# A graph attention layer and a neighbour quantile layer on one core: attention blocks of 4, 12 and 16 tiles, ordered by hand

## The chip, the core and the metric

The kernel runs on one core of a Trainium2 chip. The metric is the device time of one execution in microseconds (us), as the median of several runs. The engines of the core are TensorE (PE, matmuls; PEld is its weight load), VectorE (DVE), ScalarE (ACT), GpSimd (POOL) and SyncE (SP). Each works through its own queue of instructions in order, and waits on semaphores that the others raise. DMAs are issued from the queues of SP, ACT and POOL. A gather or scatter by a list of indices (an indirect DMA) is always issued from POOL.

## What is computed

There are 4096 nodes with 128 features, and a random adjacency matrix in which a node has about 32 neighbours. Layer 0 is a graph attention layer with eight heads; layer 1 takes quantiles over neighbours. Cut to what matters:

```python
Wh = jnp.einsum('nd,hde->hne', nodes, W)
f1 = jnp.einsum('hnd,hd->hn', Wh, a1)
f2 = jnp.einsum('hnd,hd->hn', Wh, a2)
e = leaky_relu(f1[:, :, None] + f2[:, None, :], 0.2)
att = softmax(jnp.where(adj > 0, e, -9e15), axis=-1)
h = elu(jnp.einsum('hnm,hmd->hnd', att, Wh))
x1 = layernorm(nodes + elu(concat_heads(h) @ W1 + b1)) * gamma + beta
# layer 1: of each node's neighbours every skip-th is dropped,
# the rest are sorted feature by feature
svals = jnp.sort(where(keep, x1, big), axis=1)
agg = (svals[1/4] + svals[1/2] + svals[3/4]) / 3    # places worked out from the count
out = (0.5 * agg + 0.5 * x1) @ Wl.T + bl + x1
```

Since only some 32 of the 4096 columns of a row count, the kernel makes a list of each node's neighbours and works on gathered rows.

## The kernel before

A tile is 128 nodes, so there are 32 tiles. The work has four parts.

**Search** (`neighbours`, L532). For each tile, the 128 rows of the adjacency matrix are loaded in two halves of 2048 columns (L541, a DMA of 1 MB from ACT's queue). ACT turns a half into signs in bf16 and counts them (L547). DVE multiplies each stretch of 512 by a falling ramp (L568), takes the eight largest of each 128 columns (L573), and then eight rounds of the eight largest of all candidates (L585), with these struck out after each round (L587). The result is a list of up to 64 neighbours in a record, `rec`. The function is a generator that yields after each stretch, in pieces, 12 for a tile.

**Records and ranks** (`complete_records`, `rank_by_count`). When all tiles of a block are searched, their lists are completed, all nodes of the block are ranked by their neighbour count, and the records are scattered in that order to DRAM (`rec_d`, L194, from POOL). So the tiles that attention sees have neighbours of nearly equal count, and `CAPS` holds the largest count of each.

**Attention**, tile by tile in that order. `fetch_rows` (L755) reads a tile's records back (`R`, and for narrow layers `list` and `score`, from SP's queue), lets DVE turn the lists and the f1 scores for gathering (L776 to L799), and issues one gather for each slot of the list (L185, POOL), as many as the cap rounded up to four: 24 to 64 for a tile. `weigh_rows` (L816) computes the weights (L825 to L827), spreads them (`pf`, L839), multiplies and sums the gathered rows on PE into `y` (L860), copies y to `raw` on ACT (L871), divides (L875 to L878) and transposes (`yT`, L887, L888). When 2 or 4 tiles are weighed, `transform` (L895) does the two dense layers with their ELU, and the layer norm, for them; the resulting rows `x1` are put on the list `store` and scattered to `x1_d` (L194, named x_d in the profile).

**Sort** (`quantile_out`). For each tile the x1 rows of kept neighbours are gathered, and a selection network of DVE minima and maxima (L1133) with ACT copies (L1129) finds the quantiles. It begins when all x1 rows are stored.

Attention and search overlap. The 32 tiles are handled in three blocks (`BLOCKS`), here of 2, 8 and 22. Block 0 is searched first, with nothing beside it but the set-up. While the tiles of block 0 are in attention, block 1 is searched; while block 1 is in attention, block 2 is searched; block 2 is in attention alone. The function `step` does one tile: it fetches tile i, scatters the stores that are waiting, and weighs tile i-1, with a share of the `transform` of earlier tiles and, between the yields of `weigh_rows`, a share (`quota`) of the search pieces.

What sets the order: inside `tc.manual_schedule(engines=ORDERED)`, DVE, PE and ACT run their instructions in the order in which the program writes them, and POOL's order is chosen by a planner with estimated times. This holds in blocks 0 and 1. In block 2 there is no such context, so the planner orders all engines. SP is always the planner's. The sort is ordered by hand on all engines.

Buffers that matter: gathered rows `G` have two buffers (a tile whose cap is over 44 takes two of them; the surplus over 32 of a smaller cap goes to `Gs`), and in block 2 a third, since every third is taken from another pool (`take`, L744). `R` has 5 buffers, in block 2 8. `sgn` has two, `adj_t` three. `y` has four PSUM banks (`YBANKS`), `x1` one buffer.

In block 2 the records of all tiles are scattered once more to `all_d`, in an order over all nodes, four tiles' scatters in each of the first eight steps; in the middle of the block they are read back to make the lists of the sort (`kept_rows`).

Of the kernel before, what the change touches and what calls it, by code (L numbers as in the profile page):

```python
# [9 lines left out]
F32 = mybir.dt.float32  # L10
# [7 lines left out]
ORDERED = {mybir.EngineType.DVE, mybir.EngineType.PE, mybir.EngineType.Activation}  # L18
ALL = ORDERED | {mybir.EngineType.Pool}

P = 128
# [22 lines left out]
    2: [33, 61],  # L44
    8: [27, 29, 31, 33, 34, 37, 40, 61],
    22: [
        24, 25, 26, 27, 28, 29, 30, 30, 31, 32, 32, 33, 34, 34, 35, 36, 37, 38, 39, 40, 43, 63,
    ],
# [5 lines left out]
BLOCKS = [2, 8, 22]  # L54
# [10 lines left out]
YBANKS = 4  # L65
# [143 lines left out]
def kernel(  # L209
# [132 lines left out]
    def step(fetch=None, pieces=None, quota=0, size=2, more=None):  # L342
        if fetch:
            weigh.append(fetch_rows(tc, pools, narrow[turn[0] % 2], *fetch, xt_d, bad, uses))
            turn[0] += 1
        while store:
            scatter(nc, x1_d, *store.pop(0))
        if len(weigh) > 1 or (weigh and not fetch):
            R, parts = weigh.pop(0)
            place = len(members)  # L350
            members.append(R)
            turns = len(parts) + 13
            each = -(-quota // turns)
            done = 0
            for _ in weigh_rows(tc, attp, pools, pp, parts, turned, place, size, consts):
                if tails and next(tails[0], True):
                    tails.pop(0)
                for _ in range(min(each, quota - done)):
                    next(pieces, None)
                    done += 1  # L360
            quota -= done
            if len(members) == size:
                tails.append(
                    transform(tc, attp, pp, more, turned.pop(0), list(members), consts, store)
                )
                members.clear()
        elif not fetch:
            while tails:
                if next(tails[0], True):
                    tails.pop(0)  # L370
        for _ in range(quota):
            next(pieces, None)

    t0 = 0
    for b, n in enumerate(BLOCKS):
# [5 lines left out]
        if last:  # L381
# [12 lines left out]
            for i in range(n):  # L394
                step((recs_d[b], i, CAPS[n][i], t0 + i), size=2 if i in (0, n - 1) else 4, more=kp)
                for t in waiting[:4]:
                    scatter(nc, all_d, rec[:, t, 0:REC1], ranks[:, t : t + 1])
                waiting = waiting[4:]
                if i == n // 2:
                    R = cp.tile([P, NT, REC1], F32, name="all", bufs=1)  # L400
                    nc.sync.dma_start(R, all_d.rearrange("(t p) w -> p t w", p=P))
                    kept_rows(tc, cp, R, jp1, pidx, idx, own_i, bad, limits)
                    slot_places(tc, cp, R, picks, limits)
        else:
            pieces = search(t0 + n, BLOCKS[b + 1])
            quota = -(-BLOCKS[b + 1] * PIECES // n)
            with tc.manual_schedule(engines=ORDERED):
                for i in range(n):
                    step((recs_d[b], i, CAPS[n][i], t0 + i), pieces, quota, more=kp)
                for _ in pieces:  # L410
                    pass
        t0 += n
    for _ in range(3):
        step(size=2, more=kp)
    count_bad(tc, cp, kp, bad, ones, total)
# [116 lines left out]
def neighbours(tc, adjp, rec, num, adj, tiles, back, chunk):  # L532
# [11 lines left out]
    def sign():  # L544
        t, i, cnt, adj_t = loads.pop(0)
        sgn = adjp.tile([P, half], BF16, name="sgn", bufs=2)
# [9 lines left out]
    sign()  # L556
    while signs:
# [5 lines left out]
        if i == 0:  # L563
            first = adjp.tile([P, NCH * 8], F32, name="first")
        for b in range(half // 512):

            key = sgn[:, ts(b, 512)].rearrange("p (c w) -> p c w", w=CW)
            nc.vector.tensor_tensor(  # L568
                key, key, back.unsqueeze(1).to_broadcast([P, 512 // CW, CW]), ALU.mult
            )  # L570
            c0 = i * half + b * 512
            for c in range(512 // CW):
                nc.vector.max(first[:, ts(c0 // CW + c, 8)], key[:, c, :])  # L573
            yield
# [17 lines left out]
def complete_records(tc, cp, rec, num_all, bad, jp1, pidx, t0, n):  # L592
# [3 lines left out]
    for a in range(t0, t0 + n, step):  # L596
# [12 lines left out]
        has = tmp("has")  # L609
# [134 lines left out]
def take(pools, shape, name, turn, bufs=2):  # L744
# [10 lines left out]
def fetch_rows(tc, ap, narrow, rec_d, i, cap, t, xt_d, bad, turn):  # L755
# [3 lines left out]
    R = take(ap, [P, REC], "R", turn, 5)  # L759
# [21 lines left out]
    G, col = None, 0  # L781
    for s0, w in layers(cap):
        k = P // w
        idx = ap[0].tile([P, 32], I32, name="idx", bufs=6)
# [7 lines left out]
        if w < 32 or f1x32 is None:  # L792
# [5 lines left out]
            f1x = ap[0].tile([P, 32 * H], F32, name="f1x", bufs=6)  # L798
# [3 lines left out]
        f1v = f1x.rearrange("p (h g) -> p g h", h=H)[:, 0:w, :]  # L802
        if w == 32:
# [12 lines left out]
def weigh_rows(tc, ap, pools, pp, parts, turned, place, size, consts):  # L816
# [16 lines left out]
    for half in range(2):  # L833
# [61 lines left out]
def transform(tc, ap, pp, more, yT, members, consts, store):  # L895
# [54 lines left out]
    x1 = ap.tile([P, 4, D], F32, name="x1", bufs=1)[:, 0:m, :]  # L950
# [432 lines left out]
```

## Time and profile before

| | us |
|---|---|
| median of 3 runs | 3860.11 (3859.21 to 3861.66) |
| the profiled execution, its own time | 4473.73 |
| its span, first to last instruction | 4471.8 |
| PE busy | 815.7 (18%) |
| DVE busy | 2634.2 (59%) |
| ACT busy | 1265.3 (28%) |
| POOL busy | 2284.8 (51%) |
| gathers of attention (G and Gs), POOL | 1060.0 (x1092) and 89.6 (x92) |
| gathers of the sort (vals), POOL | 911.9 (x960) |
| minima and maxima of the sort (L1133, vals), DVE | 1403.0 |

The span is from the first to the last instruction of one profiled execution. Busy time counts instructions at work, not waiting. In a line of the timeline, the first number is the start from the span's beginning, the second how long the merged instructions took; the brackets give the idle time of the engine ahead of them and what ended it: another engine's instruction, a DMA, "issue" (nothing that the profile shows), or "remote" (a semaphore whose raiser it could not name). In a line of waits stand the total in us, the number of waits, and the longest. The profiled execution is longer than the plain runs, by 613.6 us.

### The profile page before, as it was taken

Reading aid. Unit: us, or ns where it says so; the run is one execution under the profiler, and the core shown is the slowest. Engines: PE = TensorE matmul, PEld = TensorE weight load, DVE = VectorE, ACT = ScalarE, POOL = GpSimd, SP = SyncE. Lnnn points to the kernel's source line nnn. Section 1 sums busy time; section 2 is a strip of 40 time slices with the busy share of each in tenths; the row PEclk is TensorE's granted clock in tenths of the full one; section 3 lists DMA queues with packets and bytes.
Section 4 is the critical chain, followed back from the end, with each engine's and each line's share of the span. In section 5 each row is a group of like instructions: output and inputs, shape, how many; then the busy total and the mean of one; then the engine's idle time right before and its main releaser. Section 6 shows DMA issues by size and latency. Waiting matters only on the chain. (4 is left out here: it accounts for less than half of the span.)

```text
span 4471.8 us, 18412 instructions
## 1 busy us (share of the span) xinstructions
PE 815.7 (18%) x2751; PEld 469.4 (10%) x2753; DVE 2634.2 (59%) x5147; ACT 1265.3 (28%) x2352; POOL 2284.8 (51%) x2452
## 2 busy tenths in 40 slices
PE   2001212223231413332425110000000001000101
PEld 1000110111121201111112000000000000000001
DVE  5665667767111205110212436888878999999897
ACT  2112222222010213121213213333333444443433
POOL 1332343454657465756663575666565334455530
PEclk9955555555565656655656555555555555555555
DMA  5313333231222121212221111111111001111110
GB/s 168 105 48 111 97 101 96 91 93 43 54 46 53 36 57 41 55 47 48 48 51 28 40 53 39 47 45 47 40 45 41 22 21 30 31 38 35 36 28 3
DMA packets 115233, 241.18 MB, mean 54 GB/s; under 512 B 51904, under 2 KB 68288, under 8 KB 106912
## 3 DMA queue, kind: packets, MB, share of 16 engines
q0 software_dynamic: 76224, 161.01, 14.2%
q10 hardware_dynamic: 12160, 68.49, 4.5%
q1 hardware_dynamic: 26720, 10.41, 1.2%
q14 instruction: 103, 0.84, 0.1%
q8 instruction: 26, 0.43, 0.0%
HBM read 228.56 MB, written 11.18 MB: 54 GB/s over the span
## 5 line engine op out<-in xcount | busy, mean ns | idle before, releaser
L1133 DVE TENSOR_TENSOR vals<-low,vals 128x1024 f32<-128x1024 f32 (+9 forms) x1359 | 1403.0, 1058 | 338.9 <-ACT low L1129 129.8
L185 POOL DMA_INDIRECT G<-xt_d,idx x1092 | 1060.0, 971 | 736.3 <-issue 480.8
L185 POOL DMA_INDIRECT vals<-x_d,idx x960 | 911.9, 950 | 295.4 <-issue 287.5
L1129 ACT COPY low<-vals 128x1024 f32<-128x1024 f32 (+10 forms) x701 | 607.4, 876 | 968.6 <-DVE vals L1133 621.1
L871 ACT COPY raw<-y 32x129 f32<-32x129 f32 (+1 forms) x928 | 239.2, 258 | 854.6 <-remote 516.9
L860 PE MATMUL y<-G,pf 128*64 128x258 f32 (+1 forms) x1200 | 289.9, 518 | 978.3 <-issue 574.9
L1143 PE MATMUL st_ps<-ident,u 128*128 128x128 f32 x344 | 87.1, 437 | 1781.4 <-ACT u L1142 1377.9
L194 POOL DMA_INDIRECT out_dram<-o,own_i x32 | 31.8, 992 | 626.0 <-ACT o L1155 623.7
L875 DVE TENSOR_SCALAR rden<-raw 128x8 f32<-128x8 f32 x32 | 6.2, 194 | 550.5 <-ACT raw L871 407.0
L573 DVE MAX8 first<-sgn 128x8 f32<-128x128 bf16 x1024 | 223.9, 281 | 152.4 <-remote 121.5
L1143 PEld LDWEIGHTS st_ps<-ident,u 128*128 128x128 f32 x344 | 76.0, 327 | 1792.3 <-ACT u L1142 1385.4
L860 PEld LDWEIGHTS y<-G,pf 128*64 128x64 f32 (+1 forms) x1200 | 141.5, 191 | 1111.7 <-issue 861.6
L547 ACT ACTIVATE sgn<-adj_t 128x2048 bf16<-128x2048 int32 x64 | 122.1, 1907 | 303.0 <-DVE first L573 177.0
L908 DVE TENSOR_SCALAR e<-e 128x512 f32<-128x512 f32 x64 | 28.0, 437 | 242.4 <-ACT e L935 131.8
L194 POOL DMA_INDIRECT x_d<-x,R x32 | 32.9, 1027 | 260.2 <-DVE x L974 235.6
L888 ACT COPY yT<-turned 128x512 f32<-128x512 f32 x64 | 65.6, 1026 | 302.6 <-PE turned L887 157.2
L839 DVE TENSOR_TENSOR pf<-z,own 128x512 f32<-128x512 f32 x124 | 80.6, 683 | 112.1 <-issue 87.5
L887 PE MATMUL turned<-ident,raw 128*128 128x128 f32 x256 | 68.6, 420 | 391.6 <-DVE raw L878 233.1
L916 PE MATMUL o<-hv,W_sb 128*128 128x256 f32 (+1 forms) x176 | 93.8, 650 | 229.6 <-DVE hv L910 118.5
L1133 DVE TENSOR_TENSOR most<-low,most 128x1024 f32<-128x1024 f32 (+7 forms) x116 | 131.9, 1167 | 2.6 <-issue 0.5
L185 POOL DMA_INDIRECT Gs<-xt_d,idx x92 | 89.6, 974 | 85.7 <-remote 30.0
L585 DVE MAX8 rec<-first 128x8 f32<-128x256 f32 x256 | 109.3, 427 | 35.8 <-remote 18.7
(180 smaller groups left out, 1774.7 us busy)
## 6 DMA issues: line engine op xcount, KB each, us to landing
adj_t<-in_adj_dram ACTq DMA_DIRECT2D x64, 1024.0 KB
G<-xt_d,idx POOLq DMA_INDIRECT x1092
vals<-x_d,idx POOLq DMA_INDIRECT x960
R<-rec_d SPq DMA_DIRECT2D x128, 26.4 KB
xt_d<-rec SPq DMA_DIRECT2D x4, 548.0 KB
score<-rec_d SPq DMA_DIRECT2D x132, 1.0 KB
rec<-in_x_dram SPq DMA_DIRECT2D x4, 512.0 KB
Gs<-xt_d,idx POOLq DMA_INDIRECT x92
```

Of the source, the lines that this page charges most:

```text
L185: nc.gpsimd.indirect_dma_start(out=dst, out_offset=None, in_=rows, in_offset=bass.IndirectOffsetOnAxis(ap=idx, axis=0),)
L547: nc.scalar.activation(sgn, adj_t, AF.Sign, accum_out=cnt[:, i : i + 1])
L573: nc.vector.max(first[:, ts(c0 // CW + c, 8)], key[:, c, :])
L585: nc.vector.max(top, first)
L839: nc.vector.tensor_tensor(pf.rearrange("p (g k h) -> p g k h", g=g2, k=k), z[:, ts(half, g2), :].unsqueeze(2).to_broadcast(spread), own[w] ...
L860: nc.tensor.matmul(yv[p0 : p0 + m], lhsT=pf[:, c : c + m], rhs=rhs, start=(i == 0), stop=(i == len(parts) - 1), skip_group_check=True,)
L871: nc.scalar.copy(raw[p0 : p0 + m, 4 * half + b, :], yv[p0 : p0 + m, a, :])
L887: nc.tensor.transpose(t_ps[:, b, :], yn[:, 4 * half + b, :], ident)
L916: nc.tensor.matmul(o, lhsT=consts["W1_sb"][:, h, :], rhs=hv[:, ts(j, n)], start=(h == 0), stop=(h == H - 1),)
L1129: nc.scalar.copy(kept, low)
L1133: nc.vector.tensor_tensor(high if end else low, kept, high, ALU.max if end else ALU.min)
L1143: nc.tensor.matmul(st_ps, lhsT=u, rhs=ident, start=(i == 0), stop=(i == len(terms) - 1))
```

## The change

The blocks become 4, 12 and 16 tiles, with caps of their own. `fetch_rows` is split in two: `list_rows` reads the records and makes the lists on DVE, and the new `fetch_rows` only issues the gathers. The lists of tile i+1 are written ahead of the step of tile i. All four compute engines are ordered by hand, in all three blocks; the last three steps and `count_bad` are moved into the ordered part. The multiply of the search (L568) handles a half row of 2048 at once in place of four times 512. `y` takes two banks at a time, and ACT copies two of its rows in one instruction, half as many copies. `sgn` has three buffers, and two halves are signed ahead. `x1` is taken from a pool by group size; `R`, `idx` and `f1x` have more buffers; a step of `weigh_rows` has four yields fewer.

```diff
-ORDERED = {mybir.EngineType.DVE, mybir.EngineType.PE, mybir.EngineType.Activation}
-ALL = ORDERED | {mybir.EngineType.Pool}
+ALL = {
+    mybir.EngineType.DVE,
+    mybir.EngineType.PE,
+    mybir.EngineType.Activation,
+    mybir.EngineType.Pool,
+}
 CAPS = {
-    2: [33, 61],
-    8: [27, 29, 31, 33, 34, 37, 40, 61],
-    22: [
-        24, 25, 26, 27, 28, 29, 30, 30, 31, 32, 32, 33, 34, 34, 35, 36, 37, 38, 39, 40, 43, 63,
-    ],
+    4: [29, 33, 37, 63],
+    12: [25, 27, 29, 30, 31, 32, 34, 35, 36, 38, 41, 63],
+    16: [24, 26, 28, 29, 30, 31, 32, 32, 33, 34, 35, 36, 38, 39, 42, 63],
...
-BLOCKS = [2, 8, 22]
+BLOCKS = [4, 12, 16]
...
     def step(fetch=None, pieces=None, quota=0, size=2, more=None):
         if fetch:
-            weigh.append(fetch_rows(tc, pools, narrow[turn[0] % 2], *fetch, xt_d, bad, uses))
-            turn[0] += 1
+            weigh.append(fetch_rows(tc, pools, fetch, xt_d, uses))
...
-            turns = len(parts) + 13
+            turns = len(parts) + 9
...
+    def lists(b, i):
+        turn[0] += 1
+        t = sum(BLOCKS[:b]) + i
+        cap = CAPS[BLOCKS[b]][i]
+        return list_rows(tc, pools, narrow[turn[0] % 2], recs_d[b], i, cap, t, bad, uses)
...
-            for i in range(n):
-                step((recs_d[b], i, CAPS[n][i], t0 + i), size=2 if i in (0, n - 1) else 4, more=kp)
-                for t in waiting[:4]:
...
+            sizes = [2] + [4] * ((n - 2) // 4 * 4) + [2] * n
+            with tc.manual_schedule(engines=ALL):
+                ready = [lists(b, 0)]
+                for i in range(n):
+                    if i + 1 < n:
+                        ready.append(lists(b, i + 1))
+                    step(ready.pop(0), size=sizes[i], more=kp)
+                    for t in waiting[:4]:
+                        scatter(nc, all_d, rec[:, t, 0:REC1], ranks[:, t : t + 1])
...
+                for _ in range(3):
+                    step(size=2, more=kp)
+                count_bad(tc, cp, kp, bad, ones, total)
         else:
             pieces = search(t0 + n, BLOCKS[b + 1])
             quota = -(-BLOCKS[b + 1] * PIECES // n)
-            with tc.manual_schedule(engines=ORDERED):
+            with tc.manual_schedule(engines=ALL):
+                ready = [lists(b, 0)]
                 for i in range(n):
-                    step((recs_d[b], i, CAPS[n][i], t0 + i), pieces, quota, more=kp)
+                    if i + 1 < n:
+                        ready.append(lists(b, i + 1))
+                    step(ready.pop(0), pieces, quota, more=kp)
...
-        sgn = adjp.tile([P, half], BF16, name="sgn", bufs=2)
+        sgn = adjp.tile([P, half], BF16, name="sgn", bufs=3)
...
     sign()
+    if loads:
+        sign()
...
+        key = sgn.rearrange("p (c w) -> p c w", w=CW)
+        nc.vector.tensor_tensor(
+            key, key, back.unsqueeze(1).to_broadcast([P, half // CW, CW]), ALU.mult
+        )
         for b in range(half // 512):
-            key = sgn[:, ts(b, 512)].rearrange("p (c w) -> p c w", w=CW)
-            nc.vector.tensor_tensor(
-                key, key, back.unsqueeze(1).to_broadcast([P, 512 // CW, CW]), ALU.mult
-            )
             c0 = i * half + b * 512
             for c in range(512 // CW):
-                nc.vector.max(first[:, ts(c0 // CW + c, 8)], key[:, c, :])
+                nc.vector.max(first[:, ts(c0 // CW + c, 8)], key[:, b * (512 // CW) + c, :])
...
-            pool, bufs = pools[1], 8 if name == "R" else 1
+            pool, bufs = pools[1], 9 if name == "R" else 1
...
-    R = take(ap, [P, REC], "R", turn, 5)
+    R = take(ap, [P, REC], "R", turn, 7)
...
+        parts.append((s0, w, idx, f1v))
+    return R, cap, parts
+
+def fetch_rows(tc, ap, lists, xt_d, turn):
...
-            y = pp.tile([P, 512], F32, name="y", bufs=YBANKS)[:, 0 : 2 * (D + 1)]
-            yv = y.rearrange("p (a d) -> p a d", a=2)
+            if b % 2 == 0:
+                y = pp.tile([P, 2, 512], F32, name="y", bufs=2)
+            yv = y[:, b % 2, 0 : 2 * (D + 1)].rearrange("p (a d) -> p a d", a=2)
...
+            if b % 2 == 0:
+                continue
             m = P // (2 * split)
             for p0 in range(0, P, m):
-                a = p0 // m % 2
-                nc.scalar.copy(raw[p0 : p0 + m, 4 * half + b, :], yv[p0 : p0 + m, a, :])
+                a = p0 // m % 2 * (D + 1)
+                nc.scalar.copy(
+                    raw[p0 : p0 + m, 4 * half + b - 1 : 4 * half + b + 1, :],
+                    y[p0 : p0 + m, :, a : a + D + 1],
+                )
             yield
...
-    x1 = ap.tile([P, 4, D], F32, name="x1", bufs=1)[:, 0:m, :]
+    x1 = own.tile([P, m, D], F32, name=f"x1_{m}", bufs=1)
```

More of the change, by code (lines that the diff above doesn't have):

```diff
@@ L64 @@
 TURN = 12
-YBANKS = 4
 R_NUM, R_OWN, R_F1 = L, L + 1, L + 2
@@ L363, in step @@
                 tails.append(
-                    transform(tc, attp, pp, more, turned.pop(0), list(members), consts, store)
+                    transform(tc, attp, pools[0 if size == 2 else -1], pp, more, turned.pop(0), list(members), consts, store)
                 )
@@ L393 @@
             waiting = list(range(NT))
-            for i in range(n):
-                step((recs_d[b], i, CAPS[n][i], t0 + i), size=2 if i in (0, n - 1) else 4, more=kp)
-                for t in waiting[:4]:
[L397 to L403, printed above, removed]
+            sizes = [2] + [4] * ((n - 2) // 4 * 4) + [2] * n
[7 more added lines that the diff above has]
+                        scatter(nc, all_d, rec[:, t, 0:REC1], ranks[:, t : t + 1])
+                    waiting = waiting[4:]
+                    if i == n // 2:
+                        R = cp.tile([P, NT, REC1], F32, name="all", bufs=1)
+                        nc.sync.dma_start(R, all_d.rearrange("(t p) w -> p t w", p=P))
+                        kept_rows(tc, cp, R, jp1, pidx, idx, own_i, bad, limits)
+                        slot_places(tc, cp, R, picks, limits)
+                for _ in range(3):
+                    step(size=2, more=kp)
+                count_bad(tc, cp, kp, bad, ones, total)
         else:
@@ L412 @@
         t0 += n
-    for _ in range(3):
-        step(size=2, more=kp)
-    count_bad(tc, cp, kp, bad, ones, total)
     cp.release()
@@ L606, in tiny @@
             return cp.tile([P, 8], F32, name=name)[:, 0:m]
-        has = tmp("has")
+        has = tmp("c")
         nc.vector.tensor_scalar(has, keys, 0.0, None, ALU.is_gt)
@@ L750, in take, with list_rows @@
         if name == "R" or (name == "G" and turn[name] % 3 == 0):
-            pool, bufs = pools[1], 8 if name == "R" else 1
+            pool, bufs = pools[1], 9 if name == "R" else 1
     return pool.tile(shape, F32, name=name, bufs=bufs)
-def fetch_rows(tc, ap, narrow, rec_d, i, cap, t, xt_d, bad, turn):
+def list_rows(tc, ap, narrow, rec_d, i, cap, t, bad, turn):
     nc = tc.nc
-    R = take(ap, [P, REC], "R", turn, 5)
+    R = take(ap, [P, REC], "R", turn, 7)
     rows = rec_d[ts(i, P), :]
@@ L780, in fetch_rows @@
     parts = []
-    G, col = None, 0
     for s0, w in layers(cap):
-        k = P // w
-        idx = ap[0].tile([P, 32], I32, name="idx", bufs=6)
+        idx = ap[0].tile([P, 32], I32, name="idx", bufs=9)
         if w == 32:
@@ L797, in fetch_rows @@
             )
-            f1x = ap[0].tile([P, 32 * H], F32, name="f1x", bufs=6)
+            f1x = ap[0].tile([P, 32 * H], F32, name="f1x", bufs=9)
             nc.vector.transpose(f1x, f1b.rearrange("p h g -> p (h g)"))
@@ L802, in fetch_rows @@
         f1v = f1x.rearrange("p (h g) -> p g h", h=H)[:, 0:w, :]
+        parts.append((s0, w, idx, f1v))
+    return R, cap, parts
+def fetch_rows(tc, ap, lists, xt_d, turn):
+    nc = tc.nc
+    R, cap, todo = lists
+    parts = []
+    G, col = None, 0
+    for s0, w, idx, f1v in todo:
+        k = P // w
         if w == 32:
@@ L892, in weigh_rows, with transform @@
         yield
-def transform(tc, ap, pp, more, yT, members, consts, store):
+def transform(tc, ap, own, pp, more, yT, members, consts, store):
     nc = tc.nc
```

## The prediction

> **What bounds the kernel now.** I read the page first. Its chain of waits is of no use: it covers only the last 30 us. So I cut the span at four points: the first gather of the attention (94.8), of its second block (411.3), of its third (1174.7), and of the sort (2487.1), and asked for the busy time in each stretch (columns: length, then PE, PEld, DVE, ACT, POOL busy with counts, clock, DMA share, GB/s).
>
> ```profile
> 94.80:411.30 316.50, 29.03 (x122) 14.64 (x123) 201.65 (x741) 57.55 (x102) 103.15 (x108) 0.71 0.30 92
> 411.30:1174.70 763.40, 193.13 (x627) 106.11 (x626) 485.48 (x1693) 189.39 (x398) 353.17 (x356) 0.58 0.28 84
> 1174.70:2487.10 1312.40, 423.35 (x1368) 209.28 (x1368) 260.51 (x677) 261.51 (x778) 787.08 (x814) 0.61 0.20 46
> 2487.10:4471.80 1984.70, 147.69 (x536) 120.57 (x536) 1639.87 (x1823) 731.50 (x997) 1032.60 (x1086) 0.50 0.13 36
> ```
>
> Where attention runs beside the neighbour search, DVE leads and POOL stands idle more than half of the time. In the third block, 22 tiles without a search, DVE has little to do and POOL leads. The sort is DVE's, and the change does not touch it. The lines of POOL show what a gather costs and what a scatter costs behind another scatter into the same tensor:
>
> ```profile
> 1165.92 0.96 POOL L194 DMA_INDIRECT all_d<-rec,ranks  x1 [0.30 <-issue]
> 1168.39 0.96 POOL L194 DMA_INDIRECT all_d<-rec,ranks  x1 [1.51 <-DMA all_d<-rec,ranks]
> ...
> 1174.74 0.97 POOL L185 DMA_INDIRECT G<-xt_d,idx  x1 [0.30 <-issue]
> ```
>
> A gather takes 0.94 to 0.97 and a gap of 0.30, so 1.25 us; a second scatter takes 2.5. POOL's waits, first in the two searched blocks, then in the third:
>
> ```profile
> POOL x_d L194 <- DVE x L974: 124.3, 3, 50.0
> POOL G L185 <- DVE sgn L568: 65.2, 1, 65.2
> POOL G L185 <- DVE f1b L794: 54.2, 1, 54.2
> ```
> ```profile
> POOL x_d L194 <- DVE x L974: 111.3, 4, 44.1
> POOL G L185 <- PE y L860: 47.0, 3, 17.0
> POOL G L185 <- DVE f1b L794: 16.4, 2, 12.7
> ```
>
> POOL, whose order no hand sets, stands before stores whose x1 is not ready, and before gathers whose lists DVE has not made. The last view is DVE's timeline during gathers:
>
> ```profile
> 741.30 0.40 DVE L568 TENSOR_TENSOR sgn<-sgn,back 128x512 bf16<-128x512 bf16 x1
> 747.56 0.87 DVE L573 MAX8 first<-sgn 128x8 f32<-128x128 bf16 x4 [5.86 <-remote]
> 748.35 0.41 DVE L568 TENSOR_TENSOR sgn<-sgn,back 128x512 bf16<-128x512 bf16 x1
> 753.87 0.88 DVE L573 MAX8 first<-sgn 128x8 f32<-128x128 bf16 x4 [5.11 <-remote]
> ```
>
> The MAX8 needs only the line above it, yet starts 5 us late. Such late starts come in every burst of gathers, some 20 us after it begins: about 25 us of DVE for each tile. The profiled execution took 4473.7 us (span 4471.8) against a median of 3860.1, 613.6 more; I take most of that to be these late starts, so I make the sum with and without them.
>
> **The Trainium skill.** "DMA: Bandwidth & Descriptors", section "Two DMAs through the same engine are not ordered", says that a DMA depending on an earlier one must wait for its completion semaphore; the 1.51 us before the second scatter agrees. "Perfetto Trace Analysis", section "DMA Instruction — SWDGE (GPSIMD)", says that the profiled end is the end of descriptor writing, not of the transfer, so 1.25 us is POOL's cost and landing comes on top; the z of the search stage that wait for a landing G (34.3 us in three waits) fit. Price: "VectorE: DVE Perf Modes", section "The perf-mode tier table", gives 1224 ns for a bf16 tensor_tensor of 2048; here 512 take 409 ns, and no row has 2048 of this operation.
>
> **The parts, without late starts.** Gathers are the caps rounded up to four: before 100, 308 and 776 in the three blocks; after 172, 440 and 572; 1184 both times. DVE per searched tile: a block of 512 starts every 1.24 (timeline), eight of them 9.9; seven rounds of MAX8 and replace at 0.98, the last MAX8 and three small ones 1.5: 18.3. One multiply per half saves 4 x 0.44 - 1.26 = 0.52 twice: 17.2 after (at least 16.5, if the first MAX8 of each block also stops waiting for its multiply; at most 18.3, if nothing is saved). Attention's own DVE lines in the searched stretch come to 102 us for ten tiles, 10.3 each.
>
> *Start.* The first gather waits for the records of block 0. Two more tiles of search are 2 x 16 (unordered, denser) = 32, less the 6.3 that DVE waits for F at 67.7, and two more record scatters, 5: +31.
>
> *Searched blocks.* Before, DVE sets both: 8 x 18.3 + 2 x 10.3 = 167 and 22 x 18.3 + 8 x 10.3 = 485 (POOL 125 and 385), together 652. After, the first is still DVE's: 12 x 17.2 + 4 x 10.3 = 248 (POOL 215). The second becomes POOL's: 440 x 1.25 = 550 and 14 stores of x1 at 1.9 = 577 (DVE only 16 x 17.2 + 12 x 10.3 = 399). Together 825: +173. Between the blocks: before 41 (8 record scatters, R, lists) + 34 (the waits for G) + 113 (records of 22 tiles, ranks, 22 scatters) = 188. After: 12 scatters, R, two lists and the weighing of the 63-entry tile, which holds both G buffers, 97; then 80, as the search ends before POOL does but weighing now stands behind two lists on DVE: 177. Sum: +162.
>
> *Last block.* 204 fewer gathers: -255. Six fewer stores: -10. The all_d scatters, of which 16 at 1.26 lay in this stretch, now come four in a row behind each of eight tiles' gathers: 8 x (1.26 + 3 x 2.55) = 71, +51. POOL's waits for x1 inside the stretch (44 and 9) and for lists (16) go, since a store now follows a whole tile of gathers (about 45 us): -69. Sum: -283.
>
> *At nothing.* Fewer ACT copies free about 2.6 us (16 of 0.38 for 32 of 0.27; no row has 258 elements in 32 partitions, 128 x 256 takes 0.37, and the bounds are 0.27 and 0.54: 4.3 freed, or nothing) per tile of an engine that is 20% busy here; a third sgn buffer and a second early sign let ACT run ahead of DVE; without that cover ACT's waits for MAX8 (54 us in the second block) would reach DVE. Lists one tile ahead add their R and list DMAs (4, and 8 for each narrow layer) to SP one tile sooner; SP is idle enough, and a step of 45 us hides a DMA of 6. The sort: 0. Larger R, idx and f1x pools cost space alone.
>
> Total: 31 + 162 - 283 = **-90**. With late starts: the blocks' 16 bursts cost 25 each, of which POOL hides none in the first (+100) and the DVE step of the second becomes 33 + 25 = 58 against POOL's 48 (+120), where before had 234: +148 in place of +162. In the last block the tile took 56.2 before ((2411.2 - 1174.7)/22), 6.5 above POOL's work and its misplaced waits; POOL's own 810/16 = 50.6 with the same 6.5 gives 912 against 1236: -324. Total -145, a span of 4327. The median lies between; I take -120: **3740 us**.
>
> **Rivals.** *A, as above*, 3690 to 3810. For it: DVE's total work in the searched stretch hardly changes, while POOL's idle time there takes 204 gathers. Against: the second block changes its bound.
> *B, a gather costs less outside the profile.* At 1.0 us the second block is 467 (-110), the last block saves 204 in place of 255 (+51): -150, or 3710; with late starts real in plain runs as well and POOL's buffer waits gone, 3650. For it: 613 us that the profile adds.
> *C, nothing comes of it.* With two G buffers POOL waits in the second block for the matmuls of the tile before, as it does in the last (waits of 7 to 18 us at nine tiles). At 10 us in each of twelve tiles the 120 are gone: 3830 to 3870.
> *D, slower.* In the last block DVE now makes the lists of tile i+1 ahead of weighing i-1, and they wait for R. Nine R buffers just hold two groups of four and one: R of tile i+1 may load only after the stores of a group, which stand behind a tile's gathers. Behind the waiting list stand z, pf, so the matmuls, so the G buffer, so POOL. DVE has waited 31.2 us for R (at 1139). Weighing alone takes 26 (2437 to 2463), POOL's tile 45, so 19 are free; it decides when the wait passes 19 + 120/16 = 26.5 in every tile. At 31 us it costs 12 x 16 = 192: 3930. Against it: once per group it costs nothing.
>
> **Numbers.** A measurement here tells 0.2%, 7.7 us. A 0.55, B 0.20, C 0.09, D 0.16. Faster: A, B and a part of C, 0.78; same 0.05; slower: D and a little of C, 0.17. The range leaves out half of B's far end and D's: 3650 to 3880. A and B alone: 3650 to 3810.
>
> **What would show it.** Right: the sort's first gather comes 90 to 150 us sooner; first attention gather near 126; in the second block POOL's gathers follow one another with the 0.30 gap and DVE waits for G; x_d no longer waits for x inside the last block; all_d in runs of four with 1.5 us waits. Wrong: list lines (L776) waiting for R in each tile of the last block; POOL waiting for y in each tile of the second; a sort of another length.

## The result, and the profile after

The kernel after takes 3873.14 us (median of 8 runs, 3869.26 to 3879.18), the kernel before 3859.85 beside it: ratio 1.0035, interval 1.0024 to 1.0046. The change makes the kernel 13 us slower, where 120 us faster were forecast. Unchanged, on another chip, it gave 3869.45 against 3857.58: ratio 1.0032 (1.0020 to 1.0045).

One plain fact is needed for all that follows: the profile of before that stands ahead of the prediction (4473.7 us, with starts 5 us late during gathers) shows a condition that the plain runs beside it did not have, while on two chips met later it was there in every run, and the kernel before took 4427 and 4457 us. A new profile of the kernel before took 3861.33 us, span 3859.3; no MAX8 in it starts late, and none of its waits is "remote". All comparisons below are made against that profile. Its busy time by stretch, cut at the same four points as before (columns: length, then PE, PEld, DVE, ACT, POOL with counts, clock, DMA share, GB/s):

```profile
94.70:348.10 253.40, 27.41 (x123) 14.02 (x123) 199.04 (x739) 56.51 (x98) 104.76 (x109) 0.72 0.37 114
348.10:948.20 600.10, 186.94 (x628) 103.70 (x626) 487.04 (x1696) 190.25 (x403) 355.23 (x356) 0.61 0.36 107
948.20:2033.80 1085.60, 396.89 (x1368) 205.49 (x1368) 263.51 (x677) 263.77 (x778) 796.07 (x814) 0.64 0.24 56
2033.80:3859.00 1825.20, 143.39 (x536) 118.00 (x536) 1639.92 (x1823) 730.82 (x997) 1032.48 (x1086) 0.50 0.15 39
```

The same four stretches of the kernel after (span 3872.7):

```profile
122.60:473.20 350.60, 64.99 (x254) 35.49 (x255) 269.07 (x950) 84.95 (x131) 189.32 (x184) 0.69 0.39 115
473.20:1172.70 699.50, 235.20 (x859) 139.12 (x858) 414.09 (x1340) 183.34 (x328) 482.05 (x468) 0.61 0.33 91
1172.70:2047.20 874.50, 283.32 (x1054) 156.17 (x1052) 213.55 (x521) 170.15 (x359) 605.68 (x624) 0.63 0.22 52
2047.20:3872.70 1825.50, 141.06 (x536) 116.56 (x536) 1639.78 (x1823) 730.51 (x997) 1032.34 (x1086) 0.51 0.15 39
```

The start is 27.9 longer, the two searched stretches 97.2 and 99.4, the last block 211.1 shorter, the sort equal (the last window of before ends 0.3 ahead of its span): together +13.4. POOL's waits in the kernel after, in the two searched blocks (columns: total us, number, longest):

```profile
POOL G L186 <- DVE sgn L582: 61.8, 1, 61.8
...
POOL G L186 <- PE y L888: 34.4, 3, 17.7
```

and in its last block:

```profile
POOL all_d L195 <- DMA all_d<-rec,ranks: 36.9, 23, 2.8
POOL G L186 <- PE y L888: 36.0, 5, 34.8
POOL x_d L195 <- DVE tot L1064: 24.1, 1, 24.1
POOL x_d L195 <- DMA x_d<-x,R: 18.0, 11, 2.1
```

Against these, POOL's waits in the last block of the new profile of before:

```profile
POOL G L185 <- issue: 210.9, 692, 0.3
POOL x_d L194 <- DVE x L974: 28.2, 1, 28.2
...
POOL x_d L194 <- DMA x_d<-x,R: 6.5, 4, 1.9
```

This is the main reading. The kernel before has one long wait in its last block, 28.2 at its very end, for the last x1; nearly all the rest of POOL's idle time there is the 0.3 us between one indirect DMA and the next. The waits of 44, 9 and 16 us that the prediction took out of the sum do not exist in it. The kernel after has the same wait at the end (24.1), and new ones: 34.8 before its first gather, and 1.5 ahead of each all_d scatter that follows another. (In the kernel before, the planner puts all_d scatters ahead of the first gather, which then waits only the usual 0.3 us.) POOL's timeline of the kernel after:

```profile
1207.26 1.26 POOL L195 DMA_INDIRECT all_d<-rec,ranks  x1 [0.30 <-ACT e L968]
1210.02 0.96 POOL L195 DMA_INDIRECT all_d<-rec,ranks  x1 [1.50 <-DMA all_d<-rec,ranks]
...
1214.91 0.96 POOL L195 DMA_INDIRECT all_d<-rec,ranks  x1 [1.49 <-DMA all_d<-rec,ranks]
1216.18 0.97 POOL L186 DMA_INDIRECT G<-xt_d,idx  x1 [0.30 <-PE y L888]
```

### The profile page after: what moved, and what is told of

The parts are those of the page before. It is cut to its first block, busy times and chain, and to the rows that moved or that the text cites. A ratio compares the mean times of both kernels' runs of the same rounds, so it can differ in the third digit from the quotient of the medians.

```text
span 3872.7 us, 17731 instructions
## 1 busy us (share of the span) xinstructions
PE 747.5 (19%) x2799; PEld 466.1 (12%) x2801; DVE 2613.9 (67%) x4953; ACT 1204.0 (31%) x1902; POOL 2320.1 (60%) x2452
## 5 line engine op out<-in xcount | busy, mean ns | idle before, releaser
L186 POOL DMA_INDIRECT G<-xt_d,idx x1096 | 1099.1, 1003 | 470.0 <-issue 325.6
L888 PE MATMUL y<-G,pf 128*64 128x258 f32 (+1 forms) x1184 | 249.3, 492 | 837.6 <-DVE pf L866 765.1
L852 DVE TENSOR_TENSOR z<-G,f1x 128x256 f32<-128x256 f32 (+3 forms) x44 | 21.9, 498 | 418.7 <-DMA G<-xt_d,idx 411.2
L901 ACT COPY raw<-y 32x258 f32<-32x258 f32 (+1 forms) x472 | 172.2, 365 | 315.2 <-PE y L888 219.1
L854 ACT ACTIVATE z<-z 128x256 f32<-128x256 f32 (+3 forms) x60 | 20.0, 334 | 804.1 <-DVE z L853 804.1
L589 DVE MAX8 first<-sgn 128x8 f32<-128x128 bf16 x1024 | 209.5, 276 | 1.9
L195 POOL DMA_INDIRECT rec_d<-rec,ranks x32 | 30.9, 967 | 156.1 <-DVE ranks L732 100.1
L949 PE MATMUL o<-hv,W_sb 128*128 128x256 f32 (+1 forms) x208 | 85.9, 537 | 196.2 <-DVE hv L943 196.2
L1166 DVE TENSOR_TENSOR vals<-vals 128x256 f32<-128x256 f32 (+2 forms) x335 | 119.0, 410 | 0.0
```

Of the source, the lines that this page charges most:

```text
L186: nc.gpsimd.indirect_dma_start(out=dst, out_offset=None, in_=rows, in_offset=bass.IndirectOffsetOnAxis(ap=idx, axis=0),)
L195: return nc.gpsimd.indirect_dma_start(out=rows, out_offset=bass.IndirectOffsetOnAxis(ap=idx, axis=0), in_=src, in_offset=None,)
L589: nc.vector.max(first[:, ts(c0 // CW + c, 8)], key[:, b * (512 // CW) + c, :])
L888: nc.tensor.matmul(yv[p0 : p0 + m], lhsT=pf[:, c : c + m], rhs=rhs, start=(i == 0), stop=(i == len(parts) - 1), skip_group_check=True,)
L901: nc.scalar.copy(raw[p0 : p0 + m, 4 * half + b - 1 : 4 * half + b + 1, :], y[p0 : p0 + m, :, a : a + D + 1],)
L949: nc.tensor.matmul(o, lhsT=consts["W1_sb"][:, h, :], rhs=hv[:, ts(j, n)], start=(h == 0), stop=(h == H - 1),)
```

## The experiments

Times in us; each ratio is to the kernel before on the same chip.

| kernel | time | before | ratio (interval) |
|---|---|---|---|
| before, profiled anew | 3861.33 | 3858.84 | - |
| after, blocks 2, 8, 22 | 3895.10 | 3858.84 | 1.0095 (1.0078 to 1.0112) |
| before, blocks 4, 12, 16 | 3790.19 | 3858.84 | 0.9819 (0.9802 to 0.9835) |
| after, last block planned | 3809.40 | 3858.84 | 0.9869 (0.9852 to 0.9885) |
| after, all_d spread | 3844.27 | 3859.15 | 0.9960 (0.9945 to 0.9975) |
| after, last block weighs first | 3862.00 | 3859.15 | 1.0007 (0.9998 to 1.0015) |
| after, both of these | 3834.18 | 3859.15 | 0.9935 (0.9920 to 0.9950) |
| after, POOL planned | 3813.82 | 3859.15 | 0.9881 (0.9866 to 0.9897) |
| new blocks, weighing first twice | 3771.79 | 3857.58 | 0.9777 (0.9760 to 0.9793) |

**Splitting the change.** The first four kernels separate the profile, the blocks, the order, and the order of the last block.

> The kernel before once more, for a second profile. Theory 1 (the late starts and the 613 us of the first profile belong to that one execution): the profiled execution takes about 3860 us, the sort begins near 2035 and takes 1825 as in the changed kernel, and no MAX8 starts 5 us late during gathers. Theory 2 (they belong to the kernel): again about 4470, with the same late starts.

Measured: 3861.33, and a sort of 1825 in place of 1984.7. Late starts were no part of what the kernel before costs in its plain runs.

```diff
# after, with the old blocks
-BLOCKS = [4, 12, 16]
+BLOCKS = [2, 8, 22]
```

> The changed kernel with the old blocks of 2, 8 and 22: the order by hand, lists ahead and larger instructions alone. Theory 1 (each half of the change does a part, as in the prediction's sum, blocks -72, the rest -47): 3810 to 3830. Theory 2 (the order by hand costs in the last block, here 22 tiles long, what the blocks gain): over 3940. Theory 3 (the blocks cost, the rest gains): under 3800.

```diff
# before, with the new blocks, their caps, and the sizes of the groups
-BLOCKS = [2, 8, 22]
+BLOCKS = [4, 12, 16]
-                step((recs_d[b], i, CAPS[n][i], t0 + i), size=2 if i in (0, n - 1) else 4, more=kp)
+                step((recs_d[b], i, CAPS[n][i], t0 + i), size=([2] + [4] * ((n - 2) // 4 * 4) + [2] * n)[i], more=kp)
```

> The kernel before with blocks of 4, 12 and 16 and the group sizes that these need, nothing else of the change. Theory 1: about 3790. Theory 2 (blocks gain, order loses): 3750 to 3800. Theory 3 (the blocks cost): over 3900.

```diff
# after, the last block without an order by hand
-            with tc.manual_schedule(engines=ALL):
+            with ExitStack():
```

> The changed kernel with its last block left to the planner in place of the order by hand. Theory 1: 3850 to 3890, since the last block is bound by POOL's gathers either way. Theory 2 (the order by hand is what costs): under 3840.

The kernel with the old blocks lies between its theories, the blocks alone come out as expected, and the last kernel bears out its Theory 2. The blocks alone gain 69 us; everything else that the change does costs 36 with the old blocks and, with the new ones, 19 outside the last block's order and 64 in that order. So the change is a gain and a larger loss, laid over each other. With the old blocks the other parts do gain while DVE is the bound: the third block's first gather comes at 910.5 in place of 948.2. They then lose 68 between there and the sort (1154.1 against 1085.6).

**Where the last block loses.** POOL's groups, from the first record scatter of the last block to the sort (busy, mean ns, idle ahead, and what ended it). The kernel after:

```profile
L186 POOL DMA_INDIRECT G<-xt_d,idx x528 | 511.1, 968 | 195.4 <-issue 156.0 <-PE y L888 36.0 <-DMA G<-xt_d,idx 3.0
...
L195 POOL DMA_INDIRECT all_d<-rec,ranks x32 | 32.6, 1019 | 42.3 <-DMA all_d<-rec,ranks 36.9 <-issue 5.1 <-ACT e L968 0.3
L195 POOL DMA_INDIRECT x_d<-x,R x20 | 20.0, 1002 | 50.4 <-DVE tot L1064 24.1 <-DMA x_d<-x,R 18.0 <-issue 6.5
L195 POOL DMA_INDIRECT rec_d<-rec,ranks x16 | 15.4, 962 | 29.7 <-DMA rec_d<-rec,ranks 26.2 <-issue 3.5
```

The same view of the kernel before with the new blocks:

```profile
L183 POOL DMA_INDIRECT G<-xt_d,idx x528 | 513.5, 973 | 160.9 <-issue 154.5 <-DMA G<-xt_d,idx 2.7 <-DMA all_d<-rec,ranks 2.1
...
L192 POOL DMA_INDIRECT all_d<-rec,ranks x32 | 32.1, 1004 | 12.3 <-issue 8.2 <-DMA score<-rec_d 1.8 <-DMA all_d<-rec,ranks 1.7
L192 POOL DMA_INDIRECT x_d<-x,R x18 | 18.0, 1002 | 42.8 <-DVE x L972 33.7 <-issue 6.7 <-DMA x_d<-x,R 2.1
L192 POOL DMA_INDIRECT rec_d<-rec,ranks x16 | 16.0, 1000 | 23.5 <-DMA rec_d<-rec,ranks 17.6 <-issue 3.6 <-DVE hv L908 2.3
```

The busy times agree; only the idle differs: 34.5 ahead of gathers, 30.0 ahead of all_d, 7.6 ahead of x1 stores, 6.2 ahead of records. These 78 us account for the length that the kernel after has more in this part: 2047.2 - 1093.0 = 954.2 against 1963.6 - 1086.8 = 876.8, which is 77.4.

The 34.8 is at the start. POOL has scattered its last record, and DVE stands before R; the carried-over tile of 63 entries, whose rows fill both G buffers, is to be weighed behind two lists. POOL's timeline, then DVE's, of the kernel after:

```profile
1136.92 0.96 POOL L195 DMA_INDIRECT rec_d<-rec,ranks  x1 [1.70 <-DMA rec_d<-rec,ranks]
1172.70 0.98 POOL L186 DMA_INDIRECT G<-xt_d,idx  x1 [34.82 <-PE y L888]
```

```profile
1142.57 0.15 DVE L792 TENSOR_SCALAR bad<-R 128x1 f32<-128x1 f32 x1 [75.65 <-DMA R<-rec_d]
...
1160.89 0.59 DVE L852 TENSOR_TENSOR z<-G,f1x 128x256 f32<-128x256 f32 x1
```

Two edits take these causes away one at a time, and a third gives POOL alone back to the planner.

```diff
# all_d spread: one scatter behind each six gathers of a tile
             gather(nc, G[:, col + g, :], xt_d, idx[:, g : g + 1])
+            if (s0 + g) % 6 == 5 and extra:
+                scatter(nc, *extra.pop(0))
...
-                    for t in waiting[:4]:
-                        scatter(nc, all_d, rec[:, t, 0:REC1], ranks[:, t : t + 1])
```

> The kernel after, but each all_d scatter stands behind six gathers of the tile's own instead of four in a row behind all of them; same instructions, same number. Theory 1 (POOL sets the last block, and a scatter behind another into the same tensor costs it a wait of 1.6): the 32 scatters take 32 x 1.3 = 41 us in place of 74.9 (32.6 busy + 42.3 idle), so 34 less: about 3839, and the last block, 874.5 from first gather to the sort's, falls to about 840. Theory 2 (POOL's waits lie in slack that DVE's order would otherwise fill: the lists of the next tile ahead of the weighing): within 8 of 3873, with new waits for y or lists on POOL of about the 34 saved.

Measured: 3844.27, 29 under the kernel after. All 32 scatters now find the one before them landed:

```profile
L195 POOL DMA_INDIRECT all_d<-rec,ranks x32 | 32.8, 1024 | 9.7 <-issue 9.4 <-DMA G<-xt_d,idx 0.3
```

The idle falls by 32.6 and no new wait takes its place. Theory 1 holds for this part.

```diff
# last block weighs first
             with tc.manual_schedule(engines=ALL):
+                step(size=2, more=kp)
                 ready = [lists(b, 0)]
```

> The kernel after, but at the start of the last block the carried-over 63-entry tile is weighed before the lists of the block's first tile are written, not behind the first two lists; nothing else moves. Theory 1 (DVE stands 75.6 us before R, with a weighing of about 13 us behind it that holds both G buffers, so POOL waits 34.8 for y): the first gather of the last block comes about 24 us sooner (11 us behind the last record scatter, as with the new blocks alone, in place of 35.8): about 3849. Theory 2 (the first gather needs the lists anyway, and they need R): within 8 of 3873.

Measured: 3862.0, between the two theories and about half of the expected gain. POOL's timeline of this kernel shows both halves:

```profile
1063.98 1.48 POOL L186 DMA_INDIRECT G<-xt_d,idx  x1 [16.81 <-PE y L889]
...
1157.36 0.96 POOL L195 DMA_INDIRECT rec_d<-rec,ranks  x1 [1.90 <-DMA rec_d<-rec,ranks]
1167.34 0.97 POOL L186 DMA_INDIRECT G<-xt_d,idx  x1 [9.02 <-DVE f1x L814]
```

The first gather stands 9.0 behind the records, not 34.8, as Theory 1 said. But the weighing's first instruction now lies ahead of the end of the search on DVE and waits 38.7 us there for its rows; so the tile before it is weighed late, POOL stands 16.8, and the records come 21 later.

```diff
# POOL planned, in all three blocks
-            with tc.manual_schedule(engines=ALL):
+            with tc.manual_schedule(engines=ALL - {mybir.EngineType.Pool}):
```

> The kernel after with POOL's order in the three attention blocks left to the planner again; DVE, PE and ACT stay ordered by hand in all three. Theory 1 (the loss is POOL's own order in the last block, the weighing behind the lists apart): the planner puts the all_d scatters between gathers as it did before, -34 to -45, the 24 us at the start of the block stay: 3825 to 3840. Theory 2 (the loss is DVE's order: lists ahead of weighing): 3860 to 3885.

Measured: 3813.82, better than either theory had it, and within 5 of the kernel whose last block is planned on all engines. Its groups:

```profile
L186 POOL DMA_INDIRECT G<-xt_d,idx x528 | 512.3, 970 | 160.9 <-issue 157.9 <-DMA G<-xt_d,idx 1.5 <-DMA all_d<-rec,ranks 0.9
...
L195 POOL DMA_INDIRECT all_d<-rec,ranks x32 | 30.9, 965 | 31.4 <-DMA all_d<-rec,ranks 27.1 <-issue 4.3
```

Theory 1 expected the planner to spread the scatters between gathers. It did not: it put 25 of 32 between and right behind the record scatters, where POOL would else stand, at least in part, for R, the lists and y. The gathers begin at 1190.6, 18 later than in the kernel after, and have no wait left but the 0.3 us. DVE, PE and ACT keep the order by hand here, so the 59 us are what POOL's order by hand costs in all three blocks together. From the first record scatter of the last block to the sort it costs 72 (954.2 against 881.8), and ahead of that it gains 10 (the records come at 1093.0 against 1103.3). The order of the other three engines costs little there: 881.8 against 870.1 where the planner orders all four in the last block, and 4 us in the whole time.

> Both edits, all_d scatters between gathers and the carried-over tile weighed first. Theory 1: the two add up, -58: about 3815, within 10 of the kernel whose last block is left to the planner (3809). Theory 2: above 3855.

Measured: 3834.18, 39 under the kernel after, the sum of the two single gains (29 and 11), and 19 above what was expected, since weighing first brought 11, not 24, and the spread 29, not 34.

**The 19 us outside the last block's order.** With the last block planned, the kernel after still takes 19 more than the blocks alone. The second block has more than that, 639.7 from its first gather to the records against 605.2, and the first block gives 17 back (256.8 against 274.1). Of the 34.5, some 10 are waits of POOL for y. Here the planner, like the edit above, puts the first instruction of a weighing ahead of the end of the search. DVE's and POOL's timeline of the kernel whose last block is planned:

```profile
1046.33 0.60 DVE L852 TENSOR_TENSOR z<-G,f1x 128x256 f32<-128x256 f32 x1 [38.77 <-DMA G<-xt_d,idx]
1061.45 1.48 POOL L186 DMA_INDIRECT G<-xt_d,idx  x1 [16.89 <-PE y L888]
```

Six more are two x1 stores that fall into this stretch, and waits of the stores for one another. The other 18 are longer gathers, which the kernel after has as well. POOL's gathers of its second block, then those of the blocks alone:

```profile
L186 POOL DMA_INDIRECT G<-xt_d,idx x408 | 422.4, 1035 | 193.9 <-issue 121.4 <-DVE sgn L582 61.8 <-PE y L888 7.2
```

```profile
L183 POOL DMA_INDIRECT G<-xt_d,idx x408 | 404.4, 991 | 197.5 <-issue 122.0 <-PE y L858 72.5 <-DMA G<-xt_d,idx 2.1
```

The timeline of the kernel after shows when:

```profile
609.37 1.22 DVE L582 TENSOR_TENSOR sgn<-sgn,back 128x2048 bf16<-128x2048 bf16 x1
610.14 1.27 POOL L186 DMA_INDIRECT G<-xt_d,idx  x1 [0.30 <-issue]
...
618.78 1.22 DVE L582 TENSOR_TENSOR sgn<-sgn,back 128x2048 bf16<-128x2048 bf16 x1
619.19 1.62 POOL L186 DMA_INDIRECT G<-xt_d,idx  x1 [0.30 <-issue]
```

The first multiply ends at 610.59 and the gather at 611.41; the second at 620.00 and 620.81. Of the 26 gathers of this block that start during such a multiply, the median ends 0.82 behind it, and their mean is 1.41 us. With multiplies of 512 the 30 such gathers of the blocks alone end 0.83 behind too, but the multiply takes 0.41, and their mean is 1.00.

The Trainium skill, "SBUF — State Buffer", section "SBUF: two separate sides", says that VectorE and GpSimd share a port pair under an exclusive lock, and that GpSimd is shut out for the whole of a DVE instruction that runs in a two-port mode, or that has two inputs in SBUF when the GpSimd instruction reads SBUF too. The multiply has both inputs in SBUF, and a gather reads its indices there. The trace agrees: in the kernel after, an f32 multiply with both inputs in SBUF holds up a gather too, and a minimum of the sort, as long, whose input `low` lies in PSUM, does not:

```profile
637.43 1.23 DVE L911 TENSOR_TENSOR raw<-raw,rden 128x1024 f32<-128x1024 f32 x1
637.77 1.70 POOL L186 DMA_INDIRECT G<-xt_d,idx  x1 [0.30 <-issue]
...
2145.49 2.48 DVE L1166 TENSOR_TENSOR vals<-low,vals 128x1024 f32<-128x1024 f32 x2 [4.10 <-ACT low L1162]
2146.08 0.94 POOL L186 DMA_INDIRECT vals<-x_d,idx  x1 [0.30 <-issue]
```

The same holds within the sort for instructions of one shape: 11 gathers that start during a minimum or maximum over 256 elements with both inputs in SBUF, 0.3 us or more ahead of its end, take 1.14 on average; 10 that start so during one with `low` in PSUM take 0.94. The measured 0.82 is most of a gather's 0.94, so nearly all of its work seems to start when the lock is free.

Four more kernels, each run twice, price this and the weighing first. All eight runs were on the two late-starting chips, so their times can't be set against those expected, and only ratios and comparisons within a chip are used.

```diff
# big multiply: before with the new blocks, and this alone
-            nc.vector.tensor_tensor(
-                key, key, back.unsqueeze(1).to_broadcast([P, 512 // CW, CW]), ALU.mult
-            )
+        nc.vector.tensor_tensor(
+            key, key, back.unsqueeze(1).to_broadcast([P, half // CW, CW]), ALU.mult
+        )
```

> The kernel before with the new blocks, and of the other parts of the change the one multiply of 2048 per half row alone. Theory 1 (a gather that starts while DVE multiplies 2048 elements in bf16 ends only some 0.8 us behind the multiply: in the kernel after, gathers of 1.2 to 1.6 us end 0.82 behind it): the gathers of the second block, POOL's, go from a mean of 0.99 to about 1.03, +17 in all, and the first block, DVE's, gives 24 halves x 0.52 = 12 back: 3790 to 3797 in all, with the second block longer by about 15. Theory 2 (the longer gathers come from another part): the mean stays at 0.99, the 12 are a gain: about 3777.

> The new blocks alone and the multiply of 2048 once more. Gathers of the second block at a mean of 1.01 to 1.03 in place of 0.99 (+10 to +17), the first block 12 shorter: 3785 to 3797 if the multiply holds up the gathers; about 3777 if it doesn't.

Ratios 0.9686 (0.9664 to 0.9707) and 0.9688 (0.9672 to 0.9704). Gathers of the second block: mean 1.010 and 1.009. The kernel on the same two chips that has the new blocks and multiplies of 512 (weighing first, below) has 0.977 and 0.976.

Small multiply is the reverse edit, on the kernel after with its last block planned:

> The kernel after with its last block left to the planner (3809), and the multiply of 512 four times per half row again. Theory 1: the gathers of the second block go from a mean of 1.03 back to 0.99 (-17), the first block grows by 12: about 3804. Theory 2: the mean stays, the first block grows: 3821.

> The kernel after with its last block left to the planner and multiplies of 512, once more. If the multiply holds up the gathers: mean 0.98 to 0.99 in the second block, -15 there and +12 in the first, about 3806, so that the rest of the 19 us to the blocks alone lies in DVE's order at the start of the last block and in POOL's waits for x1 stores. If the multiply were all of the 19: 3790.

Ratios 0.9842 (0.9818 to 0.9866) and 0.9809 (0.9791 to 0.9827); mean 0.980 and 0.981. So the mean follows the multiply, with the other parts of the change and without them: 440 x 0.03 = 13 us of POOL here, and 440 x (1.033 - 0.989) = 19 between the kernel after and the blocks alone. That these 19 equal the 19 of the whole time is chance, since the first block, DVE's, becomes shorter (257.0 in the kernel after, 274.1 in the blocks alone). How much of that is the multiply's, and what it costs or gains in all where nothing starts late, is not measured.

**Weighing first, in both later blocks.** At the start of the second block POOL stands as well: 61.8 us in the kernel after, 58.5 with the blocks alone.

```diff
# weighing first twice: before with the new blocks, and
             with tc.manual_schedule(engines=ORDERED):
+                if weigh:
+                    step(more=kp)
                 for i in range(n):
...
             waiting = list(range(NT))
+            step(more=kp)
             for i in range(n):
```

> The kernel before with the new blocks (3790), and the carried-over tile weighed ahead of the first fetch in the second block and in the last. DVE stands 47.7 us for R at the start of the second block, then weighs between search pieces, and POOL's first gather comes 59.6 us behind the last record scatter (58.5 for y). Weighed in that stand, the first gather needs only R and the lists, 15 to 20 us behind the scatter: -35 to -45 there, at most -5 in the last block, since the planner fills that gap already: about 3750. If it only moves the wait: 3785 to 3795.

> The new blocks alone, the carried-over tile weighed ahead of the first fetch in both later blocks, once more. First gather of the second block about 10 us behind the last record scatter in place of 59.6: 3740 to 3760. If the wait only moves: 3785 to 3795.

Ratios 0.9775 (0.9754 to 0.9796) and 0.9781 (0.9765 to 0.9798). The kernel after with all four edits (all_d spread, this in both blocks, and multiplies of 512):

> The kernel after with four edits: all_d scatters between gathers, the carried-over tile weighed first in the second block and in the last (without search pieces between), and multiplies of 512. Theory: from 3834 (the first two of these, the last block alone) the start of the second block gives some 35 to 45 more, since POOL waits 61.8 us there for the carried-over tile's matmuls, which stand behind R and behind search pieces on DVE, and the multiply -5: 3785 to 3800. If the wait is set by R and the lists (last record scatter to the lists' end was 27 us with the new blocks alone), at most 35 of the 61.8 can go; if the weighing first only moves the wait, as it did in part at the start of the last block, 3825 or more.

> The kernel after with all_d scatters between gathers, the carried-over tile weighed first in both later blocks, multiplies of 512, once more: 3834 - 40 to - 50 for the second block's start, and -5 to 0 for the multiply: 3780 to 3795. If the wait only moves: above 3825.

Ratios 0.9889 (0.9860 to 0.9918) and 0.9875 (0.9851 to 0.9899). A last pair was run on a chip without late starts:

> The kernel after, unchanged. Where the kernel before takes about 3860: 3873, ratio 1.0035. Where it takes about 4430 to 4460 (late starts): the prediction's sum with late starts says -145, ratio 0.967; the last block's lost 69 us and the waits found since say at most -75, ratio 0.983 to 1.005.

> The new blocks alone, the carried-over tile weighed ahead of the first fetch in both later blocks, a third time. Where the kernel before takes about 3860: 3740 to 3760, the first gather of the second block 10 us behind the last record scatter in place of 59.6; 3785 to 3795 if the wait only moves. Where it takes about 4430 to 4460: ratio 0.978 again.

The kernel after gave 1.0032, as expected. Weighing first gave 3771.79, some 16 to 18 under the blocks alone (by ratio and by time), and is the best kernel of the study, 98 under the kernel after on the same chip. POOL's timeline at the start of the second block, the blocks alone, then with weighing first:

```profile
422.16 0.96 POOL L192 DMA_INDIRECT rec_d<-rec,ranks  x1 [1.79 <-DMA rec_d<-rec,ranks]
481.63 0.97 POOL L183 DMA_INDIRECT G<-xt_d,idx  x1 [58.52 <-PE y L858]
```

```profile
456.31 0.96 POOL L192 DMA_INDIRECT rec_d<-rec,ranks  x1 [1.72 <-DMA rec_d<-rec,ranks]
466.03 0.97 POOL L183 DMA_INDIRECT G<-xt_d,idx  x1 [8.76 <-DVE f1b L795]
```

The wait of 58.5 becomes 8.8, as expected, but the records come 34 later, for the weighing now stands ahead of part of the ranking: 15.6 are kept of 50, and the expected 3740 to 3760 was missed by 12.

## Why the prediction was wrong

**Start**, +31: right (27.9; first gather at 122.6, forecast near 126).

**Searched blocks**, +162: measured 1050.1 - 853.5 = +197. Within the blocks the bounds are right: the first is DVE's, +88 (forecast +81), the second became POOL's, +94 (forecast +92), with one wait for y of 7.2 and a 0.30 gap otherwise. The part is 35 too small all the same. Taken whole, the kernel before takes 13 more than was worked out (853.5 for 652 + 188), and the kernel after 48 more (1050.1 for 825 + 177). Of these 48, 43 lie in its second block. The price of 1224 ns for the multiply of 2048 ("VectorE: DVE Perf Modes", "The perf-mode tier table") is right, the trace has 1211; what was too small is "440 x 1.25 = 550". The same 440 take (422.4 + 32.3 + 440 x 0.30)/440 = 1.33 each, 587. Of these 37 us, 19 belong to the multiply, which was costed for DVE only; the other 18 are there with multiplies of 512 as well, where a gather takes 0.99 and not 0.95. That the +94 came out is partly luck: the kernel before had an error of the same size, 41, in its second block.

**Last block**, -283: measured -211. By its terms: gathers -267 (forecast -255), all_d +53 (forecast +51, from the pair of scatters in the profile of before: right in size and kind). Stores and POOL's waits: -10 and -69 forecast, +3 measured. This is the step that failed: "POOL's waits for x1 inside the stretch (44 and 9) and for lists (16) go". They are absent from the kernel after, but from the kernel before as well, when its starts aren't late: the new profile has no long wait there but the 28.2 for the last x1. The sum was to be one without late starts, and took them out of DVE's lines, but left POOL's waits from the same profile in. That is 69 us; 13 more are the stores, two fewer in this stretch and not six, and 18.0 us of waits for one another in place of 6.5.

**The late starts**: 30 us more were taken off (from -90 to -120) on the ground that the median lies between. It doesn't: there are none in it. (In the sum with them, the 234 of before should be 240: 316.5 + 763.4 - 652 - 188.)

These come to 82 + 35 + 30, less 3 at the start and 10 in gathers and all_d: 134, which is what lies between -120 and +13.4.

**The range and the rivals.** 3873 lies in the range, by 7 us and only because the range took in a part of D; the sign is D's, too. D's mechanism is there, but not its cost. In the last block DVE does wait for the R of a next list, and the wait ends as POOL makes the stores of a group (the first at 1555.31, with stores from 1549.7 to 1558.8):

```profile
1555.31 0.15 DVE L792 TENSOR_SCALAR bad<-R 128x1 f32<-128x1 f32 x1 [40.54 <-DMA R<-rec_d]
...
1759.30 0.15 DVE L792 TENSOR_SCALAR bad<-R 128x1 f32<-128x1 f32 x1 [34.13 <-DMA R<-rec_d]
```

These are two waits of 74.7 together, not one in each tile, and behind the first gather of the block no gather waits longer than the usual 0.3 us: once per group it costs nothing, as the argument against D had it. B is not it: a gather takes 0.97 and 0.30 without late starts too. C is not it: within the second block POOL waits for y once, 7.2. A was right on the blocks: its terms without all_d and the waits (31 + 162 - 255 - 10 = -72, or -59 without the 13 that the multiply was to save in the first block) lie about the -69 of the blocks alone. Some of that is luck: with the blocks alone the second block is 28 longer than A worked out (605 for 577), and the stretches between blocks are 31 shorter (146 for 177). What A lacked is that the order by hand had nothing to win in the last block, so that all_d's 51, which it priced, stood against nothing.

**What stays open.** Why starts were late on those chips; what the multiply of 2048 alone does to a run without late starts; and what each of the smaller parts (the y pairs, the early sign, the larger pools) does, which no run isolates.

## What to carry to other kernels

Before taking a wait out of a profile, set the profiled execution against the plain runs: where it is 16% longer, a wait in it may be the disturbance's and not the order's, so get a second profile or leave the term out. When the bound moves to a queue, order that queue last and for itself: a scatter behind another into the same tensor, and a gather behind a late weighing, cost 30.0 and 34.5 us here once POOL set the end. Test a change of several parts one part at a time: here a gain of 69 and a loss of 83 looked like no change.

## What was not expected of the hardware

A whole batch of runs can be late. On two chips, met one after the other, every run of the kernel before was about 15% longer than elsewhere (4427 and 4457 against 3859), and so was the best kernel (4327.62 and 4356.75 against 3771.79). Each of these chips was met in one batch only, so the runs don't tell whether the chip or the hour is the cause. The waits that no raiser explains sum to 1065 us over the engines in the first profile of before, and there is none in the second. On one of the late chips, the MAX8 behind the multiply waited so in the kernel with the new blocks, weighing first and multiplies of 512:

```profile
DVE first L574 <- remote: 149.9, 32, 7.4
```

With the new blocks and the big multiply, where sixteen MAX8 follow one multiply and not four, the same line comes to 9.1 and 3.9 us on the two chips, and that kernel is the fastest of the four there, 38 and 41 us under weighing first. That fewer dependent instructions are what helps is argued, not shown: the blocks alone were not run there.

And a DVE instruction holds up the indirect DMA that POOL is issuing, if both its inputs lie in SBUF: by 0.33 and 0.68 us in the two gathers shown for 1.22 us of bf16, with 0.82 us of the DMA's work left when the instruction ends. As long an instruction with one input in PSUM does not (0.94 us for the gather in the sort). Where both start within 0.04 us of each other, the gather is sometimes not held up (six times by the f32 multiply in the kernel after, 0.94 to 0.97 us for the gather).
